# A planned kernel that fills the pauses of TensorE: smaller thresholds for the fill, and fill in strips

## The chip, the cores and the metric

The kernel runs on one core of a Trainium2 chip. The metric is the device time of one execution in microseconds (us). The kernel before took 1570.38 us, the median of three runs (1570.34 to 1571.56). All data and all matrix multiplications are in 32-bit floats.

## The reference, cut to what matters

Two transformer layers act on x of shape 16 x 512 x 128 (16 batches of 512 tokens, 128 features, 16 heads of 8).

```python
xn = layernorm(x)
x = x + linear_attention(xn) + mixture_of_experts(xn)   # layer 0
xn = layernorm(x)
x = x + chunked_attention(xn) + channel_mix(xn)         # layer 1
```

- `linear_attention`: q, k, v by 128 x 128 weights, rotation of q and k by position, `elu + 1` on both, then for each token the sum of k v^T over all tokens up to it, applied to q and divided by the same sum of k.
- `mixture_of_experts`: a router gives each token 8 probabilities; the two largest, normalised, weight two of 8 experts, and one shared expert is added. An expert is `square(relu(x @ w_fc.T)) @ w_proj.T` with 512 hidden units.
- `chunked_attention`: softmax attention of chunks of 64 queries over all keys up to the end of the chunk. Each row of probabilities is scaled by a factor that a small iteration computes from its sum, and is then divided by its sum again.
- `channel_mix`: each token is mixed with the token before it, then `sigmoid(xr @ W_r.T) * (square(relu(xk @ W_k.T)) @ W_v.T)`.

## The kernel before, in words

**Tiles.** 128 partitions; a batch is 4 tiles of 128 tokens. PSUM is used as one tile `banks` of 8 banks, which the program hands out itself. The batches go in four groups of four. For a group, tokens are sent to the slots of their experts in memory by an indirect DMA of POOL (line 1223), 39 slot tiles are computed (`slot_tiles`, tiles `xg`, `xgT`, `wf`, `wp`, `hg`, `yg`), and layer 1 gathers the results back by indirect DMAs (line 1242).

**Names of the matmul rows.** `qr`, `q0m`, `k0T`, `am`, `state`, `oTs`, `o0n` belong to the linear attention; `wfc_s`, `wpj_s`, `h` to the shared expert; `qa`, `ka`, `maxima`, `ex`, `vpad`, `o1n` to the chunked attention of layer 1, in which ACT turns scores in PSUM to probabilities `ex` and DVE takes row maxima; `xp`, `xr`, `xk`, `half_wv` to the channel mix. `const_sb` holds, among others, the identity matrix for transposes and a matrix of ones.

**The planner.** The layers are not issued as they are written. Each call to an engine becomes an `Op` with an assumed cost (`COSTS`, and `cost` in `Program.call`). Generators for dispatch, expert tiles, layer 0 and layer 1 are interleaved by `PACE`. `Program.run` then plays the five engines in time: `at[name]` is the planned end of an engine's last operation, and the engine that can start earliest takes its next ready one. What comes out is a fixed order on each engine; the chip runs it with semaphores, at its own durations.

**Forms of a matmul.** `op.form` is (rows of the array, columns of the array): (128, 128) whole, (32, 128) for the scores of heads, (128, 32) for strips of 32 output columns. When the form changes, the planner charges `TURN` (138 to 208 ns). A (128, 128) matmul that comes while the form is another one is issued as four strips of 32 columns, `narrow`; in the profile these have line 331, all other operations line 326. A 128 x 128 matmul in 32-bit floats leaves two records in the trace.

**The fill.** When TensorE has a planned pause longer than `IDLE` ahead of an operation, `_keep_busy` issues matmuls that nobody reads: the identity times ones, into a bank that is free by the plan. Their number is the pause less `APART`, divided by `WARM` (224 ns) and rounded down, so that a planned rest stays open. The fill takes no time in the plan; `at["PE"]` is not moved. The only thing it changes in the plan is `self.form`. It runs on the chip in order with the rest of TensorE. In the profile of before its records have line 514.

```python
end = start + op.cost
if name == "PE" and self.warm and start - at[name] > IDLE:
    self._keep_busy(op, at[name], start - at[name] - APART)
if name == "PE":
    if self.form != (P, P) and all(part.strips for part in op.parts or [op]):
        op.form, op.narrow = (P, 32), True
    if op.form != self.form:
        end += TURN.get(op.form, 148)
        self.form = op.form
```

Of the kernel before, what the change touches and what calls it, by code (L numbers as in the profile page):

```python
# [36 lines left out]
P = 128  # L37
# [241 lines left out]

SPACE = 1900  # L280

IDLE, APART, WARM = 1000.0, 600.0, 224.0

PACE = (
    (0.1, 0.4, 0.26, 0.8, 0.0, 0.8, 0.0, 1.23),
# [5 lines left out]
class Program:  # L291
# [213 lines left out]
    def _keep_busy(self, op, begin, length):  # L505

        banks, weights, moving = self.warm
        n = int(length / WARM)
        idle = [(t, k) for t, k in banks.slots.free if t <= begin]
        if not idle or not self.form or n < 1:  # L510
            return
        _, k = min(idle)
        for _ in range(n):
            i = self.nc.tensor.matmul(
                banks.whole[:, k, 0:P], weights.made(), moving.made(), start=True, stop=True
            )
            self._behind(i.ins, self.last["PE"], mybir.DependencyClass.NoSync)
            self.last["PE"] = i.ins
        self.form = (P, P)

    def _rank(self, op):

# [1336 lines left out]
```

## Time and profile before

| | |
|---|---|
| median of three runs | 1570.38 us |
| the profiled execution: its time, its span | 1572.36 us, 1570.6 us |
| busy TensorE, matmuls | 1474.0 us, 94% |
| busy DVE, ACT, POOL | 68%, 55%, 25% |
| the fill (line 514): records, busy | 396, 52.5 us |
| mean granted clock of TensorE | 0.997 |

Busy shares are means over a long span: a first stage until about 120 us in which the layer norms and the routing of the first group start up, a long middle in which all four kinds of work are there, and an end from about 1240 us in which only layer 1 is left. Matmuls are pipelined, and the end of one in the trace is modelled; the time that a row of matmuls takes is therefore better read from its start to the start of the next row. Waits whose releaser is given as "issue" are often gaps in the records, since a few per cent of the matmul records are missing.

### The profile page before, as it was taken

The page shows a single profiled execution, that of the slowest core. Times are in us where ns is not written, and L with a number is a line of the kernel's source. Part 1 is how long each engine was busy: PE and PEld are TensorE (multiplying, and loading weights), DVE is VectorE, ACT ScalarE, POOL GpSimd, SP SyncE. Part 2 cuts the span into 40 slices and gives each one's busy share as a digit, 9 for nine tenths or more (in the row PEclk, how much of TensorE's full clock was granted, in tenths as well). Part 3 has the DMA queues.
Part 4 walks back from the last instruction along what each step waited for, and adds up shares of the span by engine and source line. Part 5 has one row for each costly group of instructions (what it writes and reads, how often), then busy time and mean ns, then how long its engine had stood idle before and what let it go on. Part 6 is the DMA issues. An engine that isn't in the chain of part 4 may idle for free. (4 is left out here: it accounts for less than half of the span.)

```text
span 1570.6 us, 53937 instructions
## 1 busy us (share of the span) xinstructions
PE 1474.0 (94%) x23232; PEld 977.6 (62%) x23232; DVE 1064.1 (68%) x2289; ACT 865.0 (55%) x1369; POOL 392.3 (25%) x425
## 2 busy tenths in 40 slices
PE   6899998999999999999999999999999989998887
PEld 5678887766666657666666666566666555444444
DVE  6864431787876777588685767586757786765763
ACT  3336464565655555655656566655665545455444
POOL 3540142342035241114400140200000521442220
PEclk9999999999999999999999999999999999999999
DMA  6247687554244554334241434431321100000000
GB/s 191 89 132 233 188 245 224 161 159 146 83 141 128 146 145 133 99 110 137 83 136 36 141 98 124 119 89 53 108 85 42 39 27 15 22 15 8 8 2 14
DMA packets 150238, 163.09 MB, mean 104 GB/s; under 512 B 12912, under 2 KB 97648, under 8 KB 150000
## 3 DMA queue, kind: packets, MB, share of 16 engines
q1 hardware_dynamic: 141808, 142.86, 30.8%
q0 software_dynamic: 8192, 16.79, 3.6%
q8 instruction: 182, 2.98, 0.8%
q14 instruction: 56, 0.46, 0.1%
HBM read 118.71 MB, written 40.89 MB: 102 GB/s over the span
## 5 line engine op out<-in xcount | busy, mean ns | idle before, releaser
L326 DVE TENSOR_REDUCE maxima<-banks 128x2 f32<-128x768 f32 (+2 forms) x448 | 385.7, 914 | 82.1 <-PE banks L326 77.2
L326 ACT ACTIVATE ex<-banks 128x1024 f32<-128x1024 f32 x320 | 311.5, 1021 | 137.7 <-PE banks L326 130.1
L326 DVE TENSOR_TENSOR am<-banks,const_sb 128x1024 f32<-128x1024 f32 x128 | 151.0, 1220 | 122.1 <-PE banks L326 118.3
L326 PE MATMUL banks<-qa,ka 32*128 32x512 f32 (+3 forms) x2048 | 194.1, 460 | 14.5 <-ACT ex L326 6.3
L1223 POOL DMA_INDIRECT rows<-xn,pl_slot x128 | 128.1, 1000 | 304.5 <-DVE pl_slot L326 173.4
L326 PE MATMUL banks<-ka,qa 32*128 32x512 f32 (+2 forms) x1792 | 185.0, 503 | 17.5 <-ACT ex L326 10.9
L1242 POOL DMA_INDIRECT back<-results,pl_slot x128 | 128.1, 1001 | 290.2 <-PE banks L326 184.0
L326 PE MATMUL banks<-ex,vpad 128*32 128x512 f32 (+3 forms) x2048 | 173.1, 439 | 0.9 <-issue 0.5
L326 PEld LDWEIGHTS banks<-qa,ka 32*128 32x128 f32 x2048 | 95.8, 183 | 91.3 <-ACT ex L326 25.6
L326 ACT ACTIVATE hg<-banks 128x512 f32<-128x512 f32 x156 | 92.9, 597 | 103.6 <-PE banks L331 80.1
L326 PEld LDWEIGHTS banks<-ka,qa 32*128 32x128 f32 x1792 | 80.4, 184 | 79.5 <-issue 20.1
L331 PE MATMUL banks<-wp,hg 128*32 128x128 f32 x3104 | 104.9, 274 | 10.2 <-issue 6.0
L326 PEld LDWEIGHTS banks<-ex,vpad 128*32 128x32 f32 x2048 | 52.6, 109 | 91.4 <-issue 64.3
L331 PE MATMUL banks<-xgT,wf 128*32 128x128 f32 x3104 | 106.0, 274 | 3.3 <-issue 1.6
L331 PEld LDWEIGHTS banks<-wp,hg 128*32 128x32 f32 x3104 | 87.5, 110 | 34.5 <-issue 21.1
L331 PEld LDWEIGHTS banks<-xgT,wf 128*32 128x32 f32 x3104 | 85.9, 110 | 27.6 <-issue 11.5
L326 ACT COPY oTs<-banks 128x256 f32<-128x256 f32 (+1 forms) x96 | 42.8, 445 | 98.7 <-PE banks L326 93.8
L326 PE MATMUL banks<-am,vpad 128*32 128x128 f32 x2048 | 82.2, 274 | 4.5 <-issue 2.0
L326 ACT ACTIVATE hg<-hg 128x1024 f32<-128x1024 f32 x80 | 83.0, 1038 | 2.5
L326 PE MATMUL banks<-q0m,k0T 32*128 32x256 f32 x1024 | 74.6, 400 | 2.3 <-ACT ex L326 1.0
L326 ACT COPY yg<-banks 128x256 f32<-128x256 f32 x80 | 29.3, 367 | 83.6 <-PE banks L331 60.4
L326 PEld LDWEIGHTS banks<-am,vpad 128*32 128x32 f32 x2048 | 59.2, 110 | 15.5 <-issue 8.3
(226 smaller groups left out, 2343.9 us busy)
## 6 DMA issues: line engine op xcount, KB each, us to landing
wf<-in_w_fc SPq DMA_DIRECT2D x156, 256.0 KB
wp<-in_w_proj SPq DMA_DIRECT2D x156, 256.0 KB
rows<-zeros SPq DMA_DIRECT2D x4, 2496.0 KB
results<-yg SPq DMA_DIRECT2D x76, 128.0 KB
xg<-rows SPq DMA_DIRECT2D x36, 256.0 KB
x_in<-in_x SPq DMA_DIRECT2D x16, 256.0 KB
x<-x SPq DMA_DIRECT2D x16, 256.0 KB
out<-rr SPq DMA_DIRECT2D x16, 256.0 KB
```

The source lines that it names most:

```text
L326: return getattr(api, method)(*map(made, args), **{k: made(a) for k, a in kw.items()})
L331: yield api.matmul(to[at : at + 32], weights[:, at : at + 32], *rest, **kw)
L1223: i = nc.gpsimd.indirect_dma_start(out=rows.made()[:, :], out_offset=bass.IndirectOffsetOnAxis(ap=slot.made(), axis=0), in_=row.made(), in ...
L1242: "POOL", lambda: nc.gpsimd.indirect_dma_start(out=o.made(), out_offset=None, in_=results.made()[:, :], in_offset=bass.IndirectOffsetOnAxi ...
```

## The change

It does three things, all to the fill.

- `IDLE` goes from 1000 to 600 ns: planned pauses between 600 and 1000 ns are filled too.
- `APART` goes from 600 to 350 ns: the planned rest left open behind a fill is 350 to 574 ns where it was 600 to 824 ns.
- Where the last operation of TensorE had the form (128, 32), the fill is issued as four strips of 32 columns and leaves the form at (128, 32). In all other cases it is whole, as before, and leaves (128, 128). The planner reads the form afterwards for the turns and for `narrow`, so its order can change.

```diff
-IDLE, APART, WARM = 1000.0, 600.0, 224.0
+IDLE, APART, WARM = 600.0, 350.0, 224.0
@@ def _keep_busy(self, op, begin, length):
         if not idle or not self.form or n < 1:
             return
         _, k = min(idle)
+        cols = self.form[1] if self.form[0] == P else P
+        self.form = (P, cols)
         for _ in range(n):
-            i = self.nc.tensor.matmul(
-                banks.whole[:, k, 0:P], weights.made(), moving.made(), start=True, stop=True
-            )
-            self._behind(i.ins, self.last["PE"], mybir.DependencyClass.NoSync)
-            self.last["PE"] = i.ins
-        self.form = (P, P)
+            for at in range(0, P, cols):
+                i = self.nc.tensor.matmul(
+                    banks.whole[at : at + cols, k, 0:P], weights.made()[:, at : at + cols],
+                    moving.made(), start=True, stop=True,
+                )
+                self._behind(i.ins, self.last["PE"], mybir.DependencyClass.NoSync)
+                self.last["PE"] = i.ins
```

## The prediction

> **What bounds the kernel now.** I read the page first, then the table of stages (windows of 40 us), then the waits of TensorE by stage, then the timeline of TensorE around the fill. From the page, engine shares and the clock over 40 slices:
>
> ```profile
> PE 1474.0 (94%) x23232; PEld 977.6 (62%) x23232; DVE 1064.1 (68%) x2289; ACT 865.0 (55%) x1369; POOL 392.3 (25%) x425
> PEclk9999999999999999999999999999999999999999
> L514 PE MATMUL banks<-const_sb 128*128 128x128 f32 x396 | 52.5, 282 | 0.1
> ```
>
> TensorE is busy 94% of the span at full clock in nearly every slice. The third line is the fill: 396 records, two to a matmul, so 198 matmuls; all lie before 300 us or after 1220 us. Two stages, as busy time of PE, PEld, DVE, ACT, POOL, then clock, DMA share, GB/s:
>
> ```profile
> 400.00:440.00 40.00, 39.76 (x608) 26.89 (x611) 36.72 (x94) 25.32 (x45) 0.00 (x0) 1.00 0.38 116
> 1240.00:1280.00 40.00, 34.80 (x564) 20.68 (x560) 27.85 (x56) 16.53 (x24) 18.87 (x22) 0.96 0.10 25
> ```
>
> From 120 to 1240 us TensorE is the bound: between 440 and 1240 us its listed waits come to 12.5 us (those called "issue" left out, which here are mostly missing records), all for ACT or DVE, which follow TensorE. A delay put in earlier therefore reaches the end. In the last 330 us it alternates with ACT and DVE, and each fill stands in a short pause. The timeline (start, length in us, what, idle before it in brackets) has what I price with:
>
> ```profile
> 43.45 6.64 PE L514 MATMUL banks<-const_sb 128*128 128x128 f32 x58
> 49.92 0.41 PE L326 MATMUL banks<-vstrips,qr 128*128 128x144 f32 x2
> ...
> 288.89 1.73 PE L514 MATMUL banks<-const_sb 128*128 128x128 f32 x14
> 290.46 1.06 PE L326 MATMUL banks<-xgT,wf 128*128 128x128 f32 x8
> ...
> 1266.58 1.15 PE L326 MATMUL banks<-ka,qa 32*128 32x384 f32 x16 [1.32 <-DVE maxima L326]
> 1269.11 1.15 PE L326 MATMUL banks<-qa,ka 32*128 32x256 f32 x16 [1.38 <-DVE maxima L326]
> 1271.41 2.09 PE L326 MATMUL banks<-ka,qa 32*128 32x384 f32 x16 [1.16 <-ACT ex L326]
> ...
> 1349.04 1.11 PE L331 MATMUL banks<-wpj_s,h 128*32 128x128 f32 x32
> 1349.91 0.45 PE L331 MATMUL banks<-small_sb,oT_a 128*32 128x128 f32 x8
> 1350.13 1.11 PE L331 MATMUL banks<-wpj_s,h 128*32 128x128 f32 x32
> 1351.16 1.15 PE L326 MATMUL banks<-ka,qa 32*128 32x384 f32 x16
> ...
> 1368.28 1.15 PE L326 MATMUL banks<-qa,ka 32*128 32x384 f32 x16 [0.45 <-DVE maxima L326]
> 1369.36 0.71 PE L514 MATMUL banks<-const_sb 128*128 128x128 f32 x4
> 1370.59 1.15 PE L326 MATMUL banks<-ka,qa 32*128 32x384 f32 x16 [0.52 <-ACT ex L326]
> ```
>
> **The price of a set.** I call one 128x128 fill matmul, or the four strips that replace it, a set. 29 sets ran from 43.45 to 49.92 us with work right behind: 6.47 / 29 = 0.223 us. Strips cost the same: 32 records of 128*32 (four sets) go from 1349.04 to 1349.91, 0.87 us, 0.218 us a set.
>
> **What the change adds.** I counted the sets in the two built instruction streams: 198 before; 235 whole and 156 strips (39 sets) after, so 274. By stage: 87 to 104 up to 131 us, 24 to 42 from there to 440 us, 87 to 128 behind. If all 76 new sets held up other work, 76 x 0.223 = 16.9 us; if each lies in a wait, nothing. Place by place:
>
> Start, +17. Thirteen go where the trace has a wait or where the work behind is not due: 0.67 (11.23, two sets, at half clock), 1.15 (29.54), 1.45 (39.92, two), 0.40 (53.19, two), 0.59 (109.03, two) and 0.68 us (130.17, two); the strip set near 61 us feeds masks (am) that DVE works off without a break from 62.4 to 67.2 us, and the set at 112.51 stands ahead of a 0.43 us wait for am whose scores are already issued. Four do not: at 21.12 (DVE had written xn_2 by 22.1, its transposes began at 23.56, right behind the fill), 43.45, 53.54 and 103.98 us the next matmul follows the fill with no idle. 4 x 0.223 = 0.9. Bounds: 0, if DVE hides all, and 6 x 0.223 = 1.3, with the two sets at 61 and 112.51 us.
>
> Middle, +18. Here the order changes too. With the strip form kept, the planner charges other turns and reorders all five engines from about 130 to 430 us (the streams differ in 51 blocks on TensorE, 36 on DVE, 40 on ACT, 6 on POOL, 12 on SP); elsewhere each keeps its order, fill aside. SP moves loads of x, xs and xg by some 15 places and POOL a few gathers; TensorE's waits of this stage name ACT and DVE, none of these queues, so I cost them at nothing; without that cover they are part of the unknown below. Five new sets stand where before has a wait behind a fill or row: 0.87 (138.60), 0.24 (148.45), 0.19 (222.28), 1.23 (236.25), 0.51 us (254.12). Three more fit the 0.30 us (287.00, ACT yg) and 0.45 us (307.57, DVE maxima) near two new places of two sets. The other ten: three between two expert tiles near 213 us, where the trace has no idle, and mainly a place near 285 us that gets 10 + 3 sets where before had 7, and those 7 already ran straight into the next matmul (288.89 to 290.46). 10 x 0.223 = 2.2. What the new order alone is worth no row shows: the waits listed for 120 to 440 us, issue left out, come to about 7 us. So it can give back at most 7 us, and I take a loss of the same size as the other end; I take 0, since the same work passes through an engine that is full on both sides.
>
> End, +41. Nearly all are one set more in front of a wait of 0.29 to 1.29 us, or one or two in a wait of 0.37 to 0.96 us that had none. 0.223 fits 0.29; two sets (0.45) in 0.29 fit with the drain of about 0.15 us that the waits do not count (a fill of 6 sets at 1399.89 to 1401.34: 1.45 - 6 x 0.223 = 0.11). Three places have no wait: before qa,ka at 871.85, at 1287.91 and at 1401.34. 3 x 0.223 = 0.7. Bounds 0 and 2.3 (a quarter of the 41 sets: 41 x 0.223 / 4).
>
> **What it removes.** Switches between shapes: a row of 32 records takes 0.87 us to a row of its own shape and 1.03 to another (1350.13 to 1351.16), so a turn costs 0.1 to 0.16. Counted in the two streams, the turns are 838 before and 838 after; strips spare turns where a whole fill would have made them, but before had no fill in most of these places. Taken at 0. The Trainium skill, "TensorEngine Tiling", section Key Properties, says that changing the tiling mode drains TensorE. By that rule strip fill is the right form, and by the counted turns the sum stays as it is.
>
> The clock: it is below full in three places, 18.6 to 22.0, 1271.4 to 1274.8 and after 1568 us. The second follows three waits of 1.16 to 1.38 us between rows, none of which the new plan fills. All pauses left open elsewhere, up to 1.38 us, kept the full clock. So no gain; bound, 3.4 us at half clock is 1.7 us. "TensorE: Matmul & The Clock Gate", section Why this matters for your kernels, asks for no idle gaps over about 3 us between bursts. By that rule too pauses of 0.6 to 1 us need no fill, which speaks against this change; the sum by it is the same.
>
> **Sum.** 0.9 + 2.2 + 0.7 = 3.8 us. The profiled execution took 1572.36 us (span 1570.6), so 1576.2 by its own time; the median of the runs shown, 1570.38, is 2.0 below it: 1574.2.
>
> **Rivals.**
> Hidden: the pauses that the planner sees are real in the new order too, and DVE and ACT set the start. For it: in before, 0.19 to 0.87 us was left behind four of the middle's five fills. Against it: the fifth had none, nor did four of the start's. Then 0 to 1.5: 1570.4 to 1572.
> Faster: the new order between 130 and 430 us takes away waits for ACT hg and yg. Half of 7 us with all fill hidden gives 1566.9. It decides for faster (under 1567.2) once over 3.1 us of these 7 go net of the fill that binds, so nearly all of them if 3.8 binds. Against it: TensorE is full behind it, and the added fill near 285 us says that the new plan waits longer there.
> A new wait: the same reorder makes TensorE wait, such as for the expert tile behind the ten sets, by up to those 7 us beside the fill: 1577 to 1582.
> That the change does nothing is excluded: the stream has 76 sets more.
>
> **How the numbers follow.** This kernel's measurement tells about 0.2% (3.1 us) from no change. Chances: my forecast with its own range 1572.5 to 1576.5, 0.42; hidden 0.30; faster 0.12; new wait 0.16. Some 0.06 of the forecast lies under 1573.5, so faster 0.12, same 0.36, slower 0.52. The range leaves out about 0.10 of each outer case: 1567.5 to 1580.
>
> **What would show it.** The fill group with 274 sets, that is 470 records of whole fill and 312 of strips; busy PE up by 10 us or more with the waits of the end shorter by 0.2 us each and the rows there in the same rhythm; TensorE at 120 us some 0.9 us behind, at 440 us about 3 behind, and that shift kept to the end; the half clock near 1271 us still there. I am wrong if the shift at 440 us is negative or over 7, if rows at the end move by more than 1 us against each other, or if fill waits for a bank (now 0.1 us in all).

## The result, and the profile after

The kernel after takes 1578.89 us, the median of five runs (1576.13 to 1583.56), against 1570.34 us in five runs of the kernel before (1569.14 to 1571.56). The ratio is 1.0051 with a 95% interval of 1.0036 to 1.0066: half a per cent slower. The profiled execution of after is its slowest one, 1583.56 us with a span of 1581.8 us.

The page of the kernel after, shares of the engines, clock over 40 slices, and the group of the fill (now line 517):

```profile
PE 1490.7 (94%) x23756; PEld 995.0 (63%) x23756; DVE 1066.4 (67%) x2289; ACT 864.9 (55%) x1369; POOL 390.4 (25%) x425
PEclk9999999999999999999999999999999999999999
L517 PE MATMUL banks<-const_sb 128*128 128x128 f32 (+1 forms) x782 | 75.9, 280 | 1.1 <-issue 1.1
```

The fill has 782 records, 470 whole and 312 of strips, as counted ahead of the run. TensorE is busy 16.7 us longer, and its share stays at 94%: the page alone can't tell whether those 16.7 us are useful, filled waits, or delay. The windows of 40 us (busy time of PE, PEld, DVE, ACT, POOL, then clock, DMA share, GB/s):

```profile
400.00:440.00 40.00, 39.72 (x560) 26.26 (x560) 35.58 (x79) 24.25 (x44) 0.00 (x0) 1.00 0.21 66
1240.00:1280.00 40.00, 35.43 (x506) 19.71 (x498) 29.74 (x59) 20.13 (x29) 22.88 (x25) 1.00 0.16 41
1280.00:1320.00 40.00, 37.66 (x496) 23.02 (x496) 33.60 (x69) 19.61 (x33) 3.51 (x5) 0.91 0.05 15
```

The stage around 420 us is as full as before. The low clock that before had near 1271 us is now behind 1280 us, and costs more there: 0.91 of a slice where it was 0.96. The timeline of TensorE after, at the places that were shown of before (start, length in us, what, idle before it in brackets):

```profile
44.98 6.86 PE L517 MATMUL banks<-const_sb 128*128 128x128 f32 x60
51.68 0.41 PE L326 MATMUL banks<-vstrips,qr 128*128 128x144 f32 x2
...
287.06 1.96 PE L331 MATMUL banks<-wp,hg 128*32 128x128 f32 x64 [0.59 <-issue]
288.83 1.49 PE L517 MATMUL banks<-const_sb 128*32 128x128 f32 x48
290.65 0.38 PE L517 MATMUL banks<-const_sb 128*32 128x128 f32 x2 [0.32 <-issue]
291.42 0.38 PE L517 MATMUL banks<-const_sb 128*32 128x128 f32 x2 [0.39 <-issue]
292.18 0.99 PE L517 MATMUL banks<-const_sb 128*32 128x128 f32 x26 [0.38 <-issue]
...
1276.13 1.15 PE L326 MATMUL banks<-ka,qa 32*128 32x384 f32 x16 [1.31 <-DVE maxima L326]
1278.66 1.15 PE L326 MATMUL banks<-qa,ka 32*128 32x256 f32 x16 [1.38 <-DVE maxima L326]
1280.96 2.09 PE L326 MATMUL banks<-ka,qa 32*128 32x384 f32 x16 [1.16 <-ACT ex L326]
...
1379.25 1.15 PE L326 MATMUL banks<-qa,ka 32*128 32x384 f32 x16 [0.23 <-DVE maxima L326]
1380.33 0.94 PE L517 MATMUL banks<-const_sb 128*128 128x128 f32 x6
1381.55 0.92 PE L326 MATMUL banks<-ka,qa 32*128 32x384 f32 x7 [0.29 <-ACT ex L326]
```

Three things are to be seen. At the end each fill goes into its wait: from the row `qa,ka` to the row `ka,qa` it was 2.31 us before (1368.28 to 1370.59) and is 2.30 us now, with the waits 0.23 us shorter. Near 1278 us nothing has changed: the three waits are still there without fill. And the ten strip sets near 289 us take from 288.83 to 292.91 us, 4.1 us where ten sets of 0.223 us would be 2.2, because the row stops three times: 0.3 to 0.4 us of idle are listed each time, and from start to start each stop is worth 0.5 to 0.7 us. The releaser of these stops is "issue".

Where the time comes from is read by the same rows in both traces. How much later each starts in the profile after: +1.5 us at 23.6 us of before (`const_sb,xn`), +2.3 at 121.3 (`wp,hg`), +4.5 at 123.2 (`const_sb,xg`, the next row), +4.3 at 126.9 (`q0T,state`, the last row ahead of the new order), +10.1 at 432.0 (`wp,hg`, the first behind it), +9.0 at 1241.7 (`qa`), +11.0 at 1282.9 (`const_sb,xn`), +11.2 at 1565.3. So the start loses 4.3 us, the stretch of new order 5.8, the longer half clock behind 1280 us about 2, and the long middle and the end next to nothing. The 2.2 us between two neighbouring rows at 121 to 123 us are a single stop, which is taken up below.

### The profile page after: what moved, and what is told of

The parts are those of the page before. It is cut to its first block, busy times and chain, and to the rows that moved or that the text cites. A ratio compares the mean times of both kernels' runs of the same rounds, so it can differ in the third digit from the quotient of the medians.

```text
span 1581.8 us, 54982 instructions
## 1 busy us (share of the span) xinstructions
PE 1490.7 (94%) x23756; PEld 995.0 (63%) x23756; DVE 1066.4 (67%) x2289; ACT 864.9 (55%) x1369; POOL 390.4 (25%) x425
## 5 line engine op out<-in xcount | busy, mean ns | idle before, releaser
L331 PE MATMUL banks<-xgT,wf 128*32 128x128 f32 x3232 | 109.9, 274 | 4.1 <-ACT hg L326 1.5
L517 PE MATMUL banks<-const_sb 128*128 128x128 f32 (+1 forms) x782 | 75.9, 280 | 1.1 <-issue 1.1
L517 PEld LDWEIGHTS banks<-const_sb 128*128 128x128 f32 (+1 forms) x782 | 67.4, 162 | 11.3 <-issue 8.1
```

The lines of the kernel that those rows point to most:

```text
L331: yield api.matmul(to[at : at + 32], weights[:, at : at + 32], *rest, **kw)
L517: i = self.nc.tensor.matmul(banks.whole[at : at + cols, k, 0:P], weights.made()[:, at : at + cols], moving.made(), start=True, stop=True,)
```

## The experiments

Theories at first. "Order": the strip form, as the planner takes it up, gives TensorE an order in which it waits. (The plan also chooses which of the kernel's own matmuls are issued in strips; the kernel after has 138 records more of these, 23 matmuls. "Order" stands for the whole plan.) "Fill": the 76 added sets hold up the work behind them. "Form": strips as such are slower than whole fill. Kernels of one group ran on one chip in five rounds beside the kernel before; the chips differ (the kernel before takes 1532.88 us on the first, 1567.85 on the second, 1570.83 on the third), so ratios are compared. The experiments leave out or add fill only, never a part of the computation. One line more at the top makes lines 326 and 331 of before 327 and 332 there, or 328 and 333, and the fill has line 520, 524 or 531.

**First group: which part of the change costs?** The constants alone, against the kernel before:

```diff
-IDLE, APART, WARM = 1000.0, 600.0, 224.0
+IDLE, APART, WARM = 600.0, 350.0, 224.0
```

> The two smaller constants alone, all fill whole (262 sets, 64 more than before; the order on DVE, ACT, POOL and SP is that of before). If added fill that binds is the price, as the prediction had it, and the order is worth nothing, this carries most of the loss: some +3 to +8 us on before (1573.5 to 1578). If the new order of 130 to 440 us is the price, this pays only for fill in the start and the end: +0.5 to +2.5 us (1571 to 1573).

Measured: 1534.28 us, ratio 1.0010 (0.9997 to 1.0023). The strips alone, against the kernel after:

```diff
-IDLE, APART, WARM = 600.0, 350.0, 224.0
+IDLE, APART, WARM = 1000.0, 600.0, 224.0
```

> The old constants with the strip form kept (204 sets, 6 more than before; the order on DVE, ACT, POOL and SP is that of after). If the added fill is the price: 6 x 0.223 us at most, so 1570 to 1572. If the new order is the price: most of the 8.5 us, 1574.5 to 1578.

Measured: 1539.16 us, ratio 1.0053 (1.0034 to 1.0071). Plan and amounts of after, but every fill issued whole:

```diff
-        cols = self.form[1] if self.form[0] == P else P
-        self.form = (P, cols)
+        cols = P
+        self.form = (P, self.form[1] if self.form[0] == P else P)
```

> After's plan with all its 274 sets, but every set issued whole: the same order on every engine and the same forms of all other matmuls, 117 fill matmuls fewer. In after's trace ten sets of strips near 289 us took 4.1 us, with stops of 0.3 to 0.4 us put down to issue. If strips starve TensorE of instructions: 1.5 to 3 us faster than after (1576 to 1577.5). If a set costs the same in both shapes, or the turns that whole fill makes weigh as much: within 1.5 us of after (1577.5 to 1580).

Measured: 1539.65 us, ratio 1.0041 (1.0026 to 1.0056). The kernel before with no fill issued at all, in the same plan and order:

```diff
-        for _ in range(n):
+        for _ in range(0):
```

> Before's plan and order with no fill issued at all. If fill that binds is what costs, taking out before's 198 sets gains in the start, where at least four places bind (9, 29, 7 and 6 sets, 11 us at most): 1560 to 1567. If fill holds the clock, pauses over 3.4 us open in the start and at the end, each stage at half clock costing up to 1.7 us, and the gain is eaten: 1568 to 1575.

Measured: 1548.3 us, ratio 1.0108 (1.0089 to 1.0126), dearer than either case had it; the mean clock is 0.973 to 0.981 in its six runs, where before has 0.993 to 1.000. So the loss of after is in the two kernels that have its order, whatever the amount and form of their fill, and not in the one that has its constants alone. "Form" doesn't explain it: the kernel with whole fill keeps the loss. Between its two expected cases that kernel does not decide: 1.0041 of 1570.34 is 1576.8 us, in the range for strips that starve TensorE, but its interval covers both, and the traces of this chip have none of the stops of 0.3 to 0.4 us inside strip fill. The fill as such is worth about 1.1%, through the clock: a straight line through the 17 runs of before on this chip gives 0.9 us for 0.001 of mean clock, so that the 0.018 between the two kernels make an estimated 16.7 us, and 15.4 were measured.

**Second group: which stretch of the order, and does the old fill of the middle bind?** The strip form changes the order in two separate stretches: strip fill planned before 200 us changes it from 131 to 230 us, strip fill planned after that from about 270 to 440 us. So they can be had one by one. First, the kernel after once more:

> The instructions of the kernel after, once more, on the chip and in the rounds of the three kernels beside it, so that these can be set against it. All theories: 1.0051 of the kernel before, inside 1.003 to 1.007, since the kernels with its order and either amount of fill gave 1.0053 and 1.0041.

Measured: 1576.0 us, ratio 1.0060 (1.0037 to 1.0082). Only the first stretch, against after (and, with `>`, only the second):

```diff
-        self.form = (P, cols)
+        self.form = (P, cols if begin < 200000 else P)
```

> The new constants, but the strip form stays in the plan only at pauses planned before 200 us, behind that the plan takes up the form (128, 128) again. So TensorE, ACT, DVE and SP have the new order from about 131 to 230 us, and the order of before from there to the end. 265 sets. Theory 'the whole order': each of the two stretches of new order costs 1 to 3 us; 1.003 of before (0.001 for the constants and 0.002 for the stretch). Rival 'one place', the loss sits behind 270 us alone, where TensorE waits for the head's chain and ex: 1.001. Rival 'fill', the added fill holds up TensorE whatever the order is: as after, 1.004 to 1.005.

Measured: 1570.52 us, ratio 1.0017 (1.0004 to 1.0030).

> The mirror of the one before: the strip form stays in the plan only at pauses planned after 200 us. The order of before up to about 270 us, the new order of all five engines from there to about 440 us. 271 sets. Theory 'the whole order': 1.003. Rival 'one place' behind 270 us: 1.005, as after; if the place lies before 230 us, 1.001. Rival 'fill': 1.004 to 1.005.

Measured: 1571.93 us, ratio 1.0030 (1.0015 to 1.0044). The kernel before without its 24 sets of the middle:

```diff
-        for _ in range(n):
+        for _ in range(0 if 120000 < begin < 600000 else n):
```

> The kernel before in plan, order and constants, but the 24 sets planned between 120 and 600 us (131 to 290 us on the chip) are not issued; 174 sets are left, nothing of the computation is left out. Theory 'the fill of the middle lies in the way of a full TensorE': up to 24 x 0.223 = 5.4 us less, 0.9965 to 0.999. Theory 'it lies in waits that are there anyway': 1.000, inside 0.998 to 1.002. Rival 'it keeps the clock': a half clock window appears between 120 and 300 us, at up to 1.7 us each, 1.001 or more.

Measured: 1568.74 us, ratio 1.0001 (0.9987 to 1.0015). The times of the two stretches, 1.0017 and 1.0030, decide little, since their intervals reach the figures of several theories. Rows behind both stretches place the costs. Against the trace of the last kernel, which has the order of before and no fill in the middle, rows at 246 to 254 us start 0.05 us earlier with the first stretch and 0.2 earlier with the second still ahead; rows at 443 to 450 us start 0.3 us earlier with the first stretch alone, and 5.5 us later with the second alone. In the kernel after, run here again, that difference grows from 4.9 to 10.7. So the second stretch costs 5.7 us, as much with and without the first. The first costs nothing that this chip shows: from the rows at 124 to 131 us, ahead of it, to those at 246 to 254 us the kernel that has it and the kernel that has not it change by the same 2.0 us against the last kernel.

It may look as if a delay of 2 us had been made good here. It was not: the last kernel, which has no fill there, runs through a window of half clock (columns as above), and its own rows fall back by 1.6 us between 137.5 and 142.8 us:

```profile
138.30:141.70 3.40, 3.40 (x18) 3.40 (x17) 2.04 (x9) 0.68 (x2) 0.00 (x0) 0.50 0.40 97
```

This is the sign that the rival "it keeps the clock" had named, and so the ratio of 1.0001 is a balance: 24 sets less, and in this profile one half clock window more.

The parts add up to less than the whole: 0.07% and 0.20% beyond the constants' 0.10% make 0.37%, at the lower end of the interval of after. The clock covers most of the gap. The runs of the two parts had a mean clock of 0.9968 and 0.9977, those of after 0.9965, those of before 0.9957. A straight line through the 29 runs of before gives 1.36 us for 0.001; at an equal clock the two parts are then an estimated 3.9 and 7.1 us slower than before, after 10.2, and the constants, read in the same way on the first chip, 2.5. 3.9 + 7.1 - 2.5 = 8.5 of 10.2 us.

On balance the 24 sets give nothing back. Among them are the 7 near 289 us of before, behind which the next matmul followed with no idle: without them that row (`xgT,wf`) starts 1.6 us earlier, the next one 0.4 us earlier, and the one behind it at the same time as before.

**Third group: the order without fill, and where the stops come from.** The kernel after without any fill in the middle:

```diff
-        for _ in range(n):
+        for _ in range(0 if 120000 < begin < 600000 else n):
```

> The kernel after, plan and order and fill, but the fill planned between 120 and 600 us (131 to about 315 us on the chip) is not issued; 230 sets are left and nothing of the computation is left out. Theory 'the order': the new order makes TensorE wait whatever fill stands in it; 1.004 to 1.006 of before, as after, and the wait for DVE xn near 291 us grows by what the fill there took. Rival 'the fill in the new order': the 13 sets near 285 us, 104 records in strips, hold up the row behind them; without them at least 4 us of the 5.6 us between 254 and 443 us go, 1.001 to 1.0025.

Measured: 1577.54 us, ratio 1.0047 (1.0034 to 1.0060). With the 44 sets gone nearly all of the loss is still there, so it is the order. Its partner on the same chip is the last experiment below, with the order of before and no fill in the middle either. The waits of TensorE from 254 to 443 us, us in total, times, longest; first with the order of before:

```profile
PE banks L332 <- issue: 3.0, 9, 0.5
PE banks L327 <- ACT hg L327: 1.6, 2, 1.4
PE banks L327 <- ACT phi L327: 1.0, 1, 1.0
PE banks L332 <- DVE maxima L327: 0.5, 1, 0.5
...
```

and with the new order:

```profile
PE banks L332 <- ACT hg L327: 5.0, 4, 2.4
PE banks L332 <- issue: 1.6, 5, 0.6
PE banks L327 <- issue: 1.4, 3, 0.9
PE banks L327 <- ACT hg L327: 1.1, 3, 0.6
PE banks L332 <- ACT ex L327: 0.8, 1, 0.8
PE banks L332 <- DVE maxima L327: 0.6, 1, 0.6
PE banks L332 <- ACT yg L327: 0.5, 1, 0.5
...
```

The waits for `hg`, the hidden units of an expert, go from 1.6 to 6.1 us, while the stops called "issue" stay at some 3 us (3.3 and 3.0 in all). In the same stretch the rows fall 4.2 us behind (0.1 us ahead at 250, 4.0 behind at 445). More than half of the growth is one wait, in the timeline of the new order without fill:

```profile
283.64 1.96 PE L332 MATMUL banks<-wp,hg 128*32 128x128 f32 x64 [0.59 <-issue]
286.09 1.08 PE L332 MATMUL banks<-xgT,wf 128*32 128x128 f32 x32 [0.49 <-ACT yg L327]
289.55 1.93 PE L332 MATMUL banks<-xgT,wf 128*32 128x128 f32 x32 [2.38 <-ACT hg L327]
```

This is where the kernel after has its ten sets. There the wait can't be seen, for the fill stands in it: in a trace with fill a lengthened wait shows up as busy TensorE. The third row also takes nearly twice as long as the second (1.93 and 1.08 us), since the clock was 0.50 from 289.2 to 292.6 us, behind the open wait. ACT's `hg` itself started 1.7 us after the matmuls it needs had ended by their modelled end, on an event whose sender the trace does not name; why ACT is late there stays open. So up to 2.6 of the 4.2 us in this trace (1.7 and 0.9) can be ACT's late start and the half clock, and neither is shown to belong to the order. That the kernel is slower does not hang on this trace: the median of its five runs is 1.0047 of before, where the partner's is 1.0007.

How much the place costs differs between chips and with the fill. From the start of that row of `wp,hg` to the start of the third row are 5.9 us here without fill, 7.7 in the kernel after, run again, and with the second stretch alone, where the strip fill stops three times, and 5.9 with 11 sets of strips in the kernel with the strips alone on the first chip, where they don't stop. So the stops of the strip fill made an estimated 1.8 us here, read across chips. And on the first chip the whole second stretch cost only 1.2 and 1.3 us (strips alone and all whole, rows at 443 to 452 us less rows at 246 to 255, against the constants alone, which stop for 1.5 us there themselves); there ACT's `hg` started within 0.1 us of the end of its matmuls. The expectation of a longer wait for `xn` was wrong: the wait is for `hg`.

The other half of the story are the stops that the profile calls "issue". Five kernels with the new constants and strip fill at the start (after, after again, the two stretches, the new order without fill) have one of 1.6 to 3.1 us near 123 us, in the same row, after 37 of its records. The timeline there, of the kernel before without its middle fill and of the one with the first new stretch:

```profile
116.54 3.75 PE L332 MATMUL banks<-xgT,wf 128*32 128x128 f32 x128
120.30 1.95 PE L332 MATMUL banks<-wp,hg 128*32 128x128 f32 x64
```

```profile
116.54 3.75 PE L332 MATMUL banks<-xgT,wf 128*32 128x128 f32 x128
120.30 1.29 PE L332 MATMUL banks<-wp,hg 128*32 128x128 f32 x37
123.34 1.06 PE L332 MATMUL banks<-wp,hg 128*32 128x128 f32 x27 [1.75 <-issue]
```

The DMA view of the latter for 121 to 122.2 us (queue, kind: packets, MB, share of 16 engines) has a reason:

```profile
q1 hardware_dynamic: 575, 0.29, 91.7%
q8 instruction: 1, 0.02, 5.0%
```

An instruction packet of 16 KB runs here, from 121.09 to 122.06 us, among data that fills the DMA engines, and the next record starts 1.28 us behind its end. This queue had 182 packets in before and 186 in after, one for 128 of TensorE's records. So a new theory: the place of a stop is fixed by the number of records ahead of it, and it opens where a dense stretch (128 records in 3.75 us here) eats the packets faster than they come. Then the fill shifts the stops by the records it adds, and the kernel before can be given the stop by padding. The edit, in before (33 sets) and in after (32 sets); `fill` is the number of sets that are issued, which the plan does not read:

```diff
+        if fill > 20 and self.padded < 33:
+            swap = min(20, 33 - self.padded)
+            self.padded += swap
+            fill -= swap
+            for _ in range(2 * swap):
+                i = self.nc.tensor.matmul(
+                    banks.whole[:, k, 0:8], weights.made(), moving.made()[:, 0:8], start=True, stop=True
+                )
...
```

> The kernel before; in its two fills of 29 sets near 32 and 43 us 33 sets are replaced by 66 matmuls of 8 columns, so that 66 more records, as many as in the kernel after, stand ahead of the first output row of an expert, wp and hg near 121 us. Theory 'instruction supply': the stop of 1.6 to 3.1 us that the kernels with the new constants have after 37 records of this row is where a 16 KB instruction packet comes too late; with the padding the kernel before gets it too, in the same row, and the next record starts 1.2 to 1.5 us behind the end of such a packet. Rival 'the fill or the new order makes it': no stop over 0.5 us in this row. The time stays within 0.2% of before in both, 0.999 to 1.002, since a delay of 2 us at 121 us was gone by 240 us in two kernels.

> The kernel after, with 64 more records ahead of 120 us in the same way (32 sets of the long fills replaced by 64 matmuls of 8 columns), half of the 128 records that an instruction packet covers. Theory 'instruction supply': the stop in the first row of wp and hg goes, and the one of 1.3 to 1.5 us in the row of ex and vpad near 371 us goes or moves too; the time is 1.002 to 1.005, up to 3 us below after. Rival: both stops stay where they are, 1.004 to 1.006.

Measured: 1588.66 us, ratio 1.0116 (1.0101 to 1.0131), and 1592.28 us, ratio 1.0137 (1.0122 to 1.0152). Both times are far from what was expected, for a reason that has nothing to do with the question: the padding ran at half clock (see the end). The stops came as the theory had them. The timeline of before with padding:

```profile
134.70 3.75 PE L333 MATMUL banks<-xgT,wf 128*32 128x128 f32 x128
138.46 1.29 PE L333 MATMUL banks<-wp,hg 128*32 128x128 f32 x37
141.62 1.06 PE L333 MATMUL banks<-wp,hg 128*32 128x128 f32 x27 [1.88 <-issue]
```

and of after with padding:

```profile
131.61 3.08 PE L333 MATMUL banks<-xgT,wf 128*32 128x128 f32 x101
135.80 0.96 PE L333 MATMUL banks<-xgT,wf 128*32 128x128 f32 x26 [1.11 <-issue]
```

With 66 more records ahead, before stops in the row of `wp,hg` after exactly 37 records, 1.42 us behind the end of an instruction packet. With 64 more, after no longer stops in that row but in the one ahead of it, after 101 records: 128 + 37 - 64 = 101. There the next record starts 1.61 us behind the end of a packet, later than the 1.2 to 1.5 us of the theory. The stop near 371 us was expected to go or move; near the same work there is one of 0.73 us in place of 1.46.

The other traces say the same without padding. The two kernels with the new constants and whole fill have their stop not in that row but in a later one, here with the constants alone:

```profile
119.44 0.28 PE L327 MATMUL banks<-wp,hg 128*128 128x128 f32 x1
122.17 1.94 PE L327 MATMUL banks<-wp,hg 128*128 128x128 f32 x15 [2.45 <-issue]
```

Counted from the start, 1369 records of TensorE stand ahead of the stop here, and the same 1369 in the kernel with all fill whole, in the five named above, in both padded kernels and in the last experiment below. Without fill it is 1113, 256 fewer, and with the strips alone 1242, 127 fewer; a packet covers 128. So it is shown that the count of records sets the place of this stop. That the dense stretch is the other condition fits, but was not tried alone: in before the same place of the row is 66 records earlier in the count, and there is no stop at record 1369, in a later row.

Read again with this, the first chip's loss in the first stretch has a cause too, in part. From 124 to 250 us the two kernels with the new order lose 3.3 and 4.6 us there against the one with the constants alone; of that 2.8 us each are stops of this kind (1.33 and 1.48 us; 0.86, 1.09, 0.43 and 0.45), of which the latter has only one of 0.26 between 123 and 262 us.

Last, a try for a better version: the order of before, the new constants at the start, no fill in the middle. The plan goes on by the old number `n`; `fill` sets are issued.

```diff
+        fill = n
+        if begin < 130000:
+            fill = int((pause - 350) / WARM) if pause > 600 else 0
+        elif begin < 600000:
+            fill = 0
```

> A try for a better version: the order of before; the new constants only for pauses planned before 130 us, no fill from there to 600 us, the old constants behind; 198 sets. Kernels with the new constants at the start had a half clock there in fewer of their profiles, and the end's 41 sets are left away. If both count, 0.998 to 0.9995; if not, 1.000, inside 0.999 to 1.001.

Measured: 1572.71 us, ratio 1.0007 (0.9996 to 1.0017). It is not better than before, and no version was found that is. It has the stop of 1.39 us behind record 1369 as well.

## Why the prediction was right, and where it was wrong

The direction and the range held: 1578.9 us lies in 1567.5 to 1580. They held by the width of the range and not by the sum, which had 3.8 us where 8.5 were measured. The likeliest case did not come, 1572.5 to 1576.5 with its 1574.2; what came is the number of the rival "a new wait", 1577 to 1582, which had 0.16. That the range reached so far was in part luck, since some of the 8.5 us are supply stops, which no case of the prediction has.

- **The new order in the middle: "I take 0".** This is the step of the sum that failed. The two ends were put at plus and minus 7 us and the value in between, on the argument that the same work passes through a full engine on both sides. Measured, the five kernels with the whole new order take 1.0041 to 1.0060 of before, whatever fill stands in it, and the three with fill in the order of before 1.0001 to 1.0010. Where it costs differs by chip: 5.7 and 5.8 us between 254 and 443 us on the second, 4.2 without fill on the third, and on the first 3.3 and 4.6 ahead of 250 us and 1.2 and 1.3 behind. What spoke for the upper end was in hand: the plan had given the place near 285 us 10 + 3 sets where it had 7, so the planner itself saw a longer pause there. It was named in the rivals and left out of the sum.
- **The middle's fill: 10 x 0.223 = 2.2 us.** Too large in the order of before, where 24 sets taken away changed nothing on balance (1.0001). "Already ran straight into the next matmul" was taken for binding; a fill that ends just as its wait does looks the same. In the new order an estimated 1.8 us at the ten sets' place are the strips', by their stops and not by their number.
- **The start: 0.9 us.** The added sets as such are hidden about as foreseen: the constants alone, with the start's and the end's sets, cost 0.10%, some 1.5 us. But the profile after is 4.3 us behind at 127 us. Of these some 2.2 are the supply stop in `wp,hg`, and 1.5 are there at 23.6 us already, behind one half clock window more than before (17 to 24 us). Neither is in the sum. As the prediction says, such a delay is kept: against the last kernel of the second group, which loses 1.6 us by its half clock in between, the two traces of after are 5.3 and 7.2 us behind at 124 to 131 us and 4.2 and 4.9 at 250. The expectation for the padded kernel before counted on a delay of 2 us being gone by 240 us in two kernels; that was the half clock window of the trace that they were compared with.
- **The waits called "issue".** They were left out as "mostly missing records". None is missing: the kernel's own records of TensorE, fill aside, are 22836 in each of five traces with the plan of before and 22974 in each of five with the plan of after, and those of `wp,hg` make 624 matmuls in both, four for each of the 156 expert tiles. So these waits are real stops: rows shift by them, the three in the ten strip sets stand in a row with all its 80 records, and the stop behind record 1369 was moved at will.
- **The end: 0.7 us.** Right within what can be read: around the fill rows keep their rhythm, waits are 0.23 us shorter. The 2 us by which rows behind 1280 us move against those before are the half clock.
- **What it removes.** Turns at 0: nothing contradicts it; fill whole or in strips differ by less than the intervals (1.0041 and 1.0053). A half clock near the three waits stayed, as said, though in two windows where there was one. That all other pauses "up to 1.38 us" kept the full clock is read too low, since 1.69 us at 1440.37 kept it too, and it holds for one execution only: the same instructions as after, run again, have a half clock from 127.3 to 130.7 us that the first trace has not.
- **The test set for the forecast** was a shift at 440 us of 0 to 7 us, and rows at the end within 1 us of each other. The profiles show 10.1 and 2, so by its own test it was wrong.

What stays open: why ACT was late at 288.9 us in the new order without fill, why the order costs at different places on different chips, and some 1.7 of the 10.2 us that after loses at an equal clock.

## What to carry to other kernels

When an edit lets a planner reorder a full engine, don't price the new order at zero: look at where the plan itself now sees a longer pause, find the wait that fills it, and remember that fill hides such a wait in a trace. Added instructions can cost more than their run time, since they move the points at which a dense stretch runs out of instructions. Before you call an "issue" stop a missing record, count the records against the program and look at the instruction packets. Before you say that a delay was made good, look for a half clock in the trace that you compare with. And fill has two sides: here 198 sets were worth 1.1% through the clock, and 64 more gained nothing.

## What the runs showed of the hardware

- **Instruction supply.** One 16 KB packet for 128 TensorE records; in all 16 "issue" stops of at least 0.5 us in the first group's traces, the next record starts 1.2 to 1.5 us behind the end of such a packet. On the slower chips that is so in 17 of 47 such stops (up to 1.61 us); what the other 30 are was not found. They occur in kernels with little fill as well: 2.1 us near 122 us with none at all.
- **A busy TensorE is not a full clock.** The padding of 8 columns kept TensorE and its weight loads busy without a gap, and the clock was half; fill of 128 columns at the same place in before ran at full clock. In the padded kernel after, the padding began at full clock, at 29.69 us, and the half clock set in at 33.4. A window of the padded kernel before (columns as above):

```profile
37.00:47.50 10.50, 10.50 (x50) 10.50 (x51) 2.11 (x10) 0.00 (x0) 0.00 (x0) 0.50 0.00 2
```

  80 records took 16.9 us, 0.21 us each, where those of 128 columns take 0.11 at full clock. "TensorE: Matmul & The Clock Gate", section Part 1: The HAM clock gate, in the Trainium skill ties the clock to how busy TensorE has been lately; here busy time by the profile was not enough, and matmuls of 128 columns kept the clock where those of 8 lost it.
- **The clock makes the spread.** The half clock comes in windows of 3.41 us, and the same program has another number of them in each execution. Among the 29 runs of before on the second chip, the two with mean clock 0.999 took 1563.5 and 1564.0 us, the three with 0.993 took 1571.3 to 1573.3: about 1.4 us per 0.001 (0.9 and 1.0 by a straight line through the runs of before on the two other chips), and one window is 3.41 x 0.5 / 1568 = 0.0011. At a clock of 0.997 the runs of before take 1566.3 to 1568.8 us and those of after 1575.4 and 1576.3.
- **Chips differ.** The kernel before took 1532.9 us on one chip and 1568 to 1571 on two others. The short stops of 0.3 to 0.4 us in dense strips, some 0.75 us apart, are on the slow ones alone; their cause was not found, and their sum (16.3 us in the trace of before, all "issue" stops counted) does not cover the difference.
